# PSUM banks ahead of the scan: seven in turn in place of three

## The chip, the core and the metric

The kernel runs on one core of a Trainium2 chip. Five engines work side by side and wait for one another through semaphores: PE (TensorE, matmuls, with its weight loads shown as PEld), DVE (VectorE), ACT (ScalarE), POOL (GpSimd) and SP (SyncE, which here only starts DMAs). Each engine takes its own instructions strictly in the order in which the program lists them. Matmul results land in PSUM, [...] a tile of 128 x 512 fills one bank. POOL works on SBUF alone in this kernel; PE writes the banks, and DVE and ACT read and write them.

The metric is device time in microseconds (us), the median of several runs. A profile is one further execution with the hardware profiler on.

## What is computed

Eight sequences of 512 tokens and 128 channels pass an adaLN-modulated Mamba2 stack of four layers, and then an adaLN-modulated mixture of eight experts (two per token, and one shared). What matters here is the Mamba part:

```python
h = _layernorm(x) * (1 + ca) + sa                # per sequence, ca and sa from a small matmul
for l in range(4):
    zxbcdt = rmsnorm(h, block_w[l]) @ W_in[l]
    z, xBC, dt = split(zxbcdt)                   # 256, 512 and 8 channels
    xBC = silu(conv_b + sum(pad(xBC)[:, k:k+L] * conv_w[:, k] for k in range(4)))
    xs, Bm, Cm = split(xBC)
    dt = softplus(dt + dt_bias);  dA = exp(dt * -exp(A_log))
    # scan over the tokens: hs = hs * dA + (dt * xs) B;  y = hs C
    h = h + rmsnorm((y + D * xs) * silu(z), gate_w) @ W_out[l]
```

## The kernel before

The scan is done in chunks of 128 tokens. A **unit** is one layer of one sequence (32 of them, layer by layer, eight sequences each); a unit has four chunks, the **items** (128 in all). One hand-written loop (L995) issues everything in program order, one pass for each value of `t`. In pass `t` item `t` is scanned, and the preparation runs ahead by 16 passes: `p = t + 16` counts the passes of preparation, with unit `v = p // 4` and block `j = p % 4`. The first pass is `t = -25` (`p = -9`); up to `t = -1` nothing is scanned, and only preparation runs. That is the stretch which the change touches.

What the preparation of a unit does, by pass:

- **Entry** (`enter`, L614, only for layer 0; a generator stepped once per pass, started at `p = 4b - 9` for sequence b). The modulation matmul into a bank `pmA` (L618), copied out by ACT (L620, L621). Statistics on DVE (L164, L166). For b = 1 to 4 the layernorm itself is on POOL (L149, L150, L172, L185, L186); for the others ACT and DVE do it. Then squares on ACT (L155), the rms factor on POOL (L149, L150), the scaled rows `hn` (POOL L201 for b = 1 to 4), the transposes into a bank `ptA` (L208), and `hT` by ACT (L210).
- **Projection** (`project_x`, L636): in each pass of the unit one block `px` of 128 channels into a bank (L640). ACT makes the first tap of the convolution out of it in the same pass (`conv_first`, L652); DVE adds the other three taps in the next pass (`conv_tap`, L662, three instructions), and only then is the bank free. I write px(v,j), first tap (v,j) and taps (v,j) below.
- `project_z` (L646): two banks `pz`, issued one pass after the unit's last block, and read by ACT one pass later (`silu`, L674, L675).
- `project_dt` (L684): bank `pdt` in the unit's second pass, read by DVE (L689).
- **Softplus** of a group of two units, written out as arithmetic on DVE: stages `softplus_a` (ACT, L697, L698), `softplus_b`, `softplus_c`, `softplus_d` (DVE, L708 to L742), of which b, c and d each take a bank as scratch (`spb`, `spc`, `spd`).
- **Sums** (`sums_a` L750 to L752 on PE into a bank `pc`; `sums_b` L758 to L769), which end with a DMA of the decays to DRAM (`crow`, L767, SP).
- The scan needs that DMA: four passes ahead of its item `decay_rows` (L781) reads `crow` back, broadcast over the partitions, into `dV`; then POOL subtracts and masks (L795, L800), and ACT takes the exponential (L811).

Besides, `prepare_experts` (L254) takes one bank (`pmods`) at `p = 0` for the modulation of the experts.

All the banks just named come from one helper, `pbank` (L504), and one pool of three banks, `psP`. The other five banks belong to the scan: `psX` one (L582; transposes and grams), `psY` two (L583; the chunk outputs `py`, L860) and `psO` two (L584; the output projection `po`, L946). A pool hands out the bank whose last reader comes earliest in the program, and the first instruction that writes the new tile waits for that reader. `psY` is first asked for at `t = 0`, `psO` at `t = 2`.

Of the kernel before, what the change touches and what calls it, by code (L numbers as in the profile page):

```python
# [8 lines left out]
F32 = mybir.dt.float32  # L9
# [6 lines left out]
P = 128  # L16
# [8 lines left out]
def adaln_mamba_moe(  # L25
# [91 lines left out]
    def load_small():  # L117
        with nc.allow_non_contiguous_dma(reason="small parameters, laid out once"):
            nc.sync.dma_start(
                dtb.rearrange("p l h -> p (l h)"),  # L120
                dt_bias.rearrange("l h -> (l h)").partition_broadcast(P),
            )
            nc.sync.dma_start(
                negA.rearrange("p l h -> p (l h)"),
                A_log.rearrange("l h -> (l h)").partition_broadcast(P),
            )
            yield
            for q in range(HB):
                nc.sync.dma_start(
                    Dch[q * HD : (q + 1) * HD],  # L130
                    D.rearrange("l (k q) -> q l k", q=HB)[q].partition_broadcast(HD),
                )
            nc.sync.dma_start(gw, gate_w.rearrange("l (k p) -> p l k", p=P))
            yield
            nc.sync.dma_start(fw, final_w.partition_broadcast(P))
            nc.sync.dma_start(nw, ffn_w.unsqueeze(1))
# [117 lines left out]
    def prepare_experts(pool):  # L254

        pm = pbank("pmods")
        nc.tensor.matmul(pm[:B, : 4 * DM], sc, wm[:, 2 * DM :], start=True, stop=True)
        pv = pm[:B, : 4 * DM].rearrange("p (k d) -> p k d", d=DM)
        mod, mag = (pool.tile([P, NH, Q], F32, tag="dV", name=n)[:, :4, :DM] for n in ("mod", "mag"))
        yield  # L260
        nc.scalar.activation(mag[:B, :2, :], pv[:, 0:4:3, :], AF.Abs)
        nc.scalar.copy(mod[:B, 1, :], pv[:, 1, :])
        nc.scalar.activation(mod[:B, 2, :], pv[:, 2, :], AF.Copy, bias=1.0)
        nc.vector.tensor_scalar(mag[:B, 2:, :], pv[:, 0:4:3, :], 0.0, 2.0, ALU.is_ge, ALU.mult)

        nc.gpsimd.iota(rank, pattern=[[-1, E]], base=E, channel_multiplier=0, **exact)
        nc.gpsimd.iota(base, pattern=[[ER, E]], base=0, channel_multiplier=0, **exact)
        yield
        nc.vector.tensor_scalar_max(mag[:B, :2, :], mag[:B, :2, :], 0.25)
        for k in range(2):  # L270
            nc.vector.scalar_tensor_tensor(
                mod[:B, 3 * k, :], mag[:B, 2 + k, :], -1.0, mag[:B, k, :], ALU.add, ALU.mult
            )
        nc.gpsimd.tensor_sub(below, upto, ident)
        nc.gpsimd.iota(tok, pattern=[[L, 2], [1, NC]], base=0, channel_multiplier=NC, **exact)
        yield
        nc.vector.tensor_mul(mod[:B, 0, :], mod[:B, 0, :], fw[:B])
        yield
        nc.sync.dma_start(mods, mod[:B])
        yield  # L280
        with nc.allow_non_contiguous_dma(reason="small parameters, laid out once"):
            nc.sync.dma_start(rwT, router_w.rearrange("e d -> d e"))
            nc.sync.dma_start(b1[:, :E, :], eb1.rearrange("e (k p) -> p e k", p=P))
            nc.sync.dma_start(b1[:, E, :], sb1.rearrange("(k p) -> p k", p=P))
        nc.sync.dma_start(b2, sb2.partition_broadcast(P))
        yield
# [213 lines left out]
    psP = front.enter_context(tc.tile_pool(name="psP", bufs=3, space=PSUM))  # L500

    wip = front.enter_context(tc.tile_pool(name="wip", bufs=2, side="right"))

    def pbank(name):  # L504
        return psP.tile([P, 512], F32, tag="p", name=name)

    banks.append(pbank)

# [63 lines left out]
    with ExitStack() as actx:  # L572
# [10 lines left out]
        psY = actx.enter_context(tc.tile_pool(name="psY", bufs=2, space=PSUM))  # L583
        psO = actx.enter_context(tc.tile_pool(name="psO", bufs=2, space=PSUM))  # L584
# [22 lines left out]
        def load_x(b):  # L607
            if b % 2 == 0:
                xp[b // 2] = fx.tile([P, 2, NC, DM], F32, tag="x", name=f"x{b}")
                hp[b // 2] = stay.tile([P, 2, NC, DM], F32, tag="h", name=f"h{b}")  # L610
            xs[b] = xp[b // 2][:, b % 2]
            nc.sync.dma_start(xs[b], x[b].rearrange("(s p) d -> p s d", p=P))
# [379 lines left out]
                    del gens[key]  # L992

        EARLY = 9
        for t in range(-NC * LEAD - EARLY, NI + 4):  # L995
            p = t + NC * LEAD
            drain = p >= NI
            if 0 <= p + EARLY < B:
                load_x(p + EARLY)
            if p == 4 - EARLY:  # L1000
                gens["small"] = load_small()
            if p == 0:
                gens["experts"] = prepare_experts(df)
            if t == 2 * NC:
                gens["lists"] = clear_lists()
            if t == NI - LEAD * NC + 2:
                for k, w in enumerate((sw1, sw2.rearrange("(k p) o -> p k o", p=P))):
                    w12.append(wip.tile([P, NPROJ], F32, tag="Wi", name=f"ws{k}")[:, :FH])
                    dst = w12[k] if k == 0 else w12[k].rearrange("p (k o) -> p k o", o=DM)
                    nc.sync.dma_start(dst, w)  # L1010
            for g, seqs in enumerate(sets):
                if t == NC * (U - B) + NC * (seqs[-1] + 1) + 2:
                    gens["pairs", g] = rejoin(g)
            v, j = divmod(p, NC)
            vc, jc = divmod(p - 1, NC)

            if (p + 2 * NC) % (NC * B) == 0 and unit(p // NC + 2):
                load_weights((p // NC + 2) // B)
            if p % (NC * B) == NC and unit(v):
                scale_weights(v // B)  # L1020
            if p == NC:
                nc.scalar.activation(negA, negA, AF.Exp)
                nc.scalar.mul(negA, negA, -1.0)
            if (p + EARLY) % NC == 0 and 0 <= (p + EARLY) // NC < B:
                gens[(p + EARLY) // NC] = enter((p + EARLY) // NC)
            if t % NC == 3 and unit(t // NC - 1) and t // NC - 1 + B < U:
                gens[t // NC - 1 + B] = renorm(t // NC - 1)

            if item(t + 4):
                decay_rows(t + 4)  # L1030
            vz, jz = divmod(p - 5, NC)
            if jz == 0 and unit(vz):
                silu(vz)
            if item(t + 2):
                decay_exp(t + 2)

            if item(t):
                state_out(t)
            if item(t - 1):
                chunk_out(t - 1)  # L1040
            if item(t):
                state_decay(t)
            if item(t + 1):
                weigh(t + 1)
            if drain and scatters and item(t + 3):
                scatter(*scatters.pop(0)[1:])
            if item(t):
                mix(t)
            if item(t - 3):
                out_add(t - 3)  # L1050
            if item(t):
                state_next(t)
            if drain:
                step_pairs()
            if item(t - 1):
                gate(t - 1)
                square(t - 1)
            if item(t - 2):
                project_out(t - 2)
            if item(t + 1):  # L1060
                gram(t + 1)
            if item(t + 2):
                transposes(t + 2)
            if item(t + 3):
                decay_diff(t + 3)
                decay_mask(t + 3)
            if unit(vc):
                conv_tap(vc, jc, 1)
            if item(t - 2):
                out_scale(t - 2)  # L1070
            if unit(vc):
                conv_tap(vc, jc, 2)
                conv_tap(vc, jc, 3)
                px.pop((vc, jc))
            for key in list(gens):
                if not step(gens[key]):
                    del gens[key]
            if drain and routed:
                serve()
            group_stages(p, ((sums_a, 7),))  # L1080
            if j == 1 and unit(v):
                project_dt(v)
            group_stages(p, ((softplus_a, 2), (softplus_b, 3), (softplus_c, 5), (softplus_d, 6), (sums_b, 7)))
            if unit(v):
                project_x(v, j)
                conv_first(v, j)
            if j == 0 and unit(v - 1):
                project_z(v - 1)
# [135 lines left out]
    with tc.manual_schedule(engines={*tc.nc.engines} - {mybir.EngineType.Pool}):  # L1224
# [48 lines left out]
        for b in range(B):  # L1273
# [3 lines left out]
            y = y1[b].rearrange("p (s d) -> p s d", d=DM)  # L1277
# [56 lines left out]
```

## Time and profile before

| | us |
|---|---|
| median of three runs (1149.92 to 1153.31) | 1150.44 |
| the profiled execution, as timed | 1151.86 |
| its span, from the first to the last instruction | 1150.2 |

Busy time in the span, by engine and by stage (us from the span's start):

| stage | length | PE | DVE | ACT | POOL |
|---|---|---|---|---|---|
| 0 to 23, loads and the first entries | 23 | 7.7 | 5.6 | 8.4 | 15.0 |
| 23 to 50, units 0 and 1 | 27 | 16.1 | 19.4 | 18.3 | 24.0 |
| 50 to 77, units 2 and 3, softplus and sums of the first group | 27 | 20.7 | 20.7 | 18.6 | 12.0 |
| 77 to 105, last passes of preparation, first items | 28 | 15.2 | 17.2 | 17.9 | 26.3 |
| 200 to 700, the scan | 500 | 460.3 | 433.4 | 417.7 | 436.7 |
| 830 to 1150, experts and output | 320 | 254.5 | 172.6 | 110.9 | 155.4 |

The first matmul of item 0 (L872) starts at 88.89. How to read the views used later: a line of the waits says which engine and line waited, for whom, and then the total in us, the number of times and the longest. A line of the timeline has the start, the duration of the merged run, engine, line, operation, the tiles written and read, how many instructions were merged (x3), and in brackets how long the engine was idle before it, and who ended that.

### The profile page before, as it was taken

How to read it: one execution, taken by the hardware profiler on the slowest of the kernel's cores; microseconds unless marked ns; L12 is line 12 of the kernel's file. 1: busy time of each engine (PE TensorE's matmuls, PEld its weight loads, DVE VectorE, ACT ScalarE, POOL GpSimd, SP SyncE). 2: the span in 40 equal slices, each digit the busy share in tenths (PEclk: the TensorE clock that was granted, in tenths of full speed). 3: DMA queues.
4: the chain of work that ended last, by engine and by line, in shares of the span. 5: the costliest groups of instructions: out<-in, count | busy, mean ns of one | idle time of the engine just before them, and what ended most of it. 6: DMA issues, size and time to landing. Idle time of an engine off the chain costs nothing. (4 is left out here: it accounts for less than half of the span.)

```text
span 1150.2 us, 21566 instructions
## 1 busy us (share of the span) xinstructions
PE 967.3 (84%) x7130; PEld 732.4 (64%) x7130; DVE 859.0 (75%) x2084; ACT 761.5 (66%) x1641; POOL 856.3 (74%) x937
## 2 busy tenths in 40 slices
PE   3666899989999989999998999879664994999995
PEld 1234666767677667676676676657453674888882
DVE  2858888888988888888889888887764652666653
ACT  3766888878898788888978887876534741333320
POOL 6858879888898798988988988989666163555550
PEclk9777989999999999999999999986886896999998
DMA  5131436455475454653432433423201015788856
GB/s 110 4 128 49 136 98 195 130 157 176 112 227 153 127 183 135 184 170 100 128 109 88 140 109 125 134 91 129 85 27 37 9 45 160 222 231 224 220 145 226
DMA packets 134302, 151.19 MB, mean 131 GB/s; under 512 B 22568, under 2 KB 106696, under 8 KB 134192
## 3 DMA queue, kind: packets, MB, share of 16 engines
q1 hardware_dynamic: 127184, 137.91, 40.6%
q0 software_dynamic: 4672, 9.42, 2.4%
q10 hardware_dynamic: 2336, 2.50, 0.7%
q8 instruction: 56, 0.92, 0.3%
q14 instruction: 54, 0.44, 0.1%
HBM read 120.07 MB, written 29.71 MB: 130 GB/s over the span
## 5 line engine op out<-in xcount | busy, mean ns | idle before, releaser
L662 DVE SCALAR_TENSOR_TENSOR xbc<-px,cw,xbc 128x511 f32<-128x511 f32 (+2 forms) x384 | 286.2, 745 | 36.4 <-ACT xbc L652 29.3
L795 POOL TENSOR_TENSOR dV<-dV,cum 128x1024 f32<-128x1024 f32 x128 | 243.8, 1905 | 5.5 <-DMA dV<-crow 5.5
L854 DVE TENSOR_TENSOR dV<-dV,ptx 128x1024 f32<-128x1024 f32 x128 | 155.1, 1211 | 18.7 <-ACT xT L832 18.7
L800 POOL TENSOR_SCALAR_AFFINE_SELECT dV<-dV 128x1024 f32<-128x1024 f32 x128 | 142.6, 1114 | 9.3
L811 ACT ACTIVATE dV<-dV 128x1024 f32<-128x1024 f32 x128 | 134.5, 1051 | 15.6 <-POOL dV L800 15.3
L487 POOL DMA_INDIRECT yg<-y,ix x78 | 84.1, 1079 | 79.3 <-DVE y L1220 64.7
L938 ACT ACTIVATE sq<-g 128x256 f32<-128x256 f32 x128 | 53.0, 414 | 119.5 <-DVE g L934 105.6
L640 PE MATMUL px<-hT,Wi 128*128 128x512 f32 x192 | 104.9, 629 | 15.8 <-DVE xbc L662 14.5
L652 ACT ACTIVATE xbc<-px,cbias,cw 128x512 f32<-128x512 f32 x128 | 98.4, 769 | 23.3 <-PE px L640 21.9
L838 POOL TENSOR_TENSOR xd<-xT,dt 128x256 f32<-128x256 f32 x128 | 79.5, 621 | 29.4 <-ACT xT L832 28.8
L487 POOL DMA_INDIRECT xg<-row,ix x64 | 63.3, 990 | 50.4 <-ACT hds L523 29.7
L863 PEld LDWEIGHTS py<-xbc,st 128*128 128x128 f32 x384 | 60.3, 204 | 60.6 <-issue 47.4
L953 PE MATMUL po<-Wo,g 128*128 128x128 f32 x512 | 88.9, 297 | 0.0
L1202 ACT ACTIVATE hd<-ph,bs 128x256 f32<-128x256 f32 x78 | 32.7, 470 | 84.1 <-PE ph L1196 81.7
L922 PE MATMUL py<-dV,xd 128*32 128x128 f32 x2048 | 84.5, 284 | 0.0
L949 PEld LDWEIGHTS po<-ones,sq 128*128 128x128 f32 x512 | 67.7, 192 | 26.1 <-issue 23.2
L912 PEld LDWEIGHTS py<-xbc,dg 128*128 128x128 f32 x512 | 79.3, 201 | 7.0 <-issue 1.0
L850 PE MATMUL ptx<-xbc 128*128 128x128 f32 x256 | 56.0, 301 | 32.6 <-DVE dV L854 32.0
L912 PE MATMUL py<-xbc,dg 128*128 128x128 f32 x512 | 81.4, 284 | 0.0
L949 PE MATMUL po<-ones,sq 128*128 128x1 f32 x512 | 78.2, 257 | 0.5 <-ACT sq L938 0.5
L1209 PE MATMUL pe<-w,hd 128*128 128x128 f32 x624 | 75.9, 275 | 0.0
L1196 PE MATMUL ph<-xt,w 128*128 128x256 f32 x312 | 75.8, 388 | 0.0
(252 smaller groups left out, 2348.8 us busy)
## 6 DMA issues: line engine op xcount, KB each, us to landing
dV<-crow SPq DMA_DIRECT2D x128, 512.0 KB, 4.0
w<-in_L_ffn_ew_dram SPq DMA_DIRECT2D x78, 256.0 KB, 3.5
xg<-blank SPq DMA_DIRECT2D x64, 260.0 KB, 4.7
ecum<-crow SPq DMA_DIRECT2D x256, 48.0 KB, 3.2
rows<-xg SPq DMA_DIRECT2D x39, 130.0 KB, 3.2
b<-in_L_ffn_eb_dram SPq DMA_DIRECT2D x39, 64.0 KB, 4.5
x<-in_L_attn_x_dram SPq DMA_DIRECT2D x8, 256.0 KB, 5.4
md<-mods SPq DMA_DIRECT2D x8, 256.0 KB, 4.9
```

What stands on the lines that cost most here:

```text
L487: i = nc.gpsimd.indirect_dma_start(out=to, out_offset=bass.IndirectOffsetOnAxis(ap=ix, axis=0), in_=of, in_offset=None)
L640: nc.tensor.matmul(px[v, k][:, :L], Wi[l][:, c0 : c0 + P], hT[v], start=True, stop=True)
L652: nc.scalar.activation(xbc[v][:, k, :], px[v, k][:, :L], AF.Identity, bias=cbias[:, l, k : k + 1], scale=cw[:, l, k, KT - 1 : KT],)
L662: nc.vector.scalar_tensor_tensor(xbc[v][:, k, d:], px[v, k][:, : L - d], cw[:, l, k, KT - 1 - d : KT - d], xbc[v][:, k, d:], ALU.mult, ALU ...
L795: nc.gpsimd.tensor_tensor(dV[i], dV[i], cums[g][:, h0 : h0 + NH].unsqueeze(2).to_broadcast([P, NH, Q]), ALU.subtract)
L800: nc.gpsimd.affine_select(out=dV[i], in_=dV[i], pattern=[[0, NH], [1, Q]], compare_op=ALU.is_ge, fill=-200.0, base=0, channel_multiplier=-1,)
L811: nc.scalar.activation(dV[i], dV[i], AF.Exp)
L854: nc.vector.tensor_mul(Ms[i], Ms[i], pg.pop(i).unsqueeze(1).to_broadcast([P, NH, Q]))
L912: nc.tensor.matmul(py[i][:, k, :], dg[l][:, k, :], xbc[u][:, k, t], start=False, stop=True, skip_group_check=True,)
L922: nc.tensor.matmul(py[i][j * HD : (j + 1) * HD, k, :], xd[:, h, :], M[:, h, :], start=False, stop=True, skip_group_check=True,)
L949: nc.tensor.matmul(pp[:, 2 * DM + c : 2 * DM + c + 1], sq[:, k, :], ones[:, 0:1], start=(k == 0), stop=(k == NB - 1))
L953: nc.tensor.matmul(pp[:, c * DM : (c + 1) * DM], g[:, k, :], Wo[l][:, k, :], start=(k == 0), stop=(k == NB - 1))
```

## The change

`pbank` looks at a list, `spare`. While the list holds entries, it takes the pool at its head, gives the tile that pool's tag, and moves the entry to the end. The list is filled just before the loop with P, Y, O, P, Y, O, P (for `psP`, `psY`, `psO`), so the three, two and two banks of these pools are asked for in a fixed turn of seven. It is emptied at the start of pass `t = -3` (`p = 13`); from there on every bank comes from `psP` as before. No arithmetic, no instruction and no order of instructions on an engine differs; what differs is the bank that a tile lies in, and so which earlier reader its writer waits for.

```diff
+    spare = []
+
     def pbank(name):
-        return psP.tile([P, 512], F32, tag="p", name=name)
+        pool, tag = psP, "p"
+        if spare:
+            pool, tag = spare[0]
+            spare.append(spare.pop(0))
+        return pool.tile([P, 512], F32, tag=tag, name=name)
...
         EARLY = 9
+        three = ((psP, "p"), (psY, "y"), (psO, "o"))
+        spare.extend((*three, *three, three[0]))
         for t in range(-NC * LEAD - EARLY, NI + 4):
             p = t + NC * LEAD
             drain = p >= NI
+            if t == -3:
+                spare.clear()
```

## The prediction

> **What bounds the kernel now.** Only the passes before t = -3 change, so I read the 40 slices first, then the waits of each engine from 23 to 77.3 us, then the timelines of DVE, ACT and POOL there.
>
> From the page's slices (28.8 us each, busy share in tenths):
>
> ```profile
> DVE  2858888888988888888889888887764652666653
> POOL 6858879888898798988988988989666163555550
> ```
>
> POOL is at 6, 8, 5, 8 in the first four slices: nearly full from 29 to 58, half empty from 58 to 86. So the stretch has two halves with different limits. The waits of 23 to 77.3:
>
> ```profile
> PE px L640 <- DVE xbc L662: 8.1, 3, 4.7
> PE pdt L684 <- ACT mdA L621: 3.3, 1, 3.3
> ...
> ACT xbc L652 <- PE px L640: 9.2, 6, 4.0
> ACT unread L155 <- POOL h L186: 3.3, 2, 2.9
> ...
> POOL dtd L769 <- ACT edec L765: 6.8, 1, 6.8
> POOL dV L795 <- DMA dV<-crow: 5.5, 1, 5.5
> ```
>
> PE does wait for banks: a new px for the taps that still read an old one, and ACT then waits for that px. But ACT also waits for POOL's layernorm, and the last two rows are the hole of the second half: POOL sits idle until the first group's sums reach it, first as edec, then through DRAM as dV. POOL's timeline gives the places:
>
> ```profile
> 50.87 0.19 POOL L149 TENSOR_SCALAR rrA<-ssA 128x4 f32<-128x4 f32 x1 [1.83 <-ACT unread L155]
> ...
> 61.97 1.27 POOL L186 TENSOR_TENSOR h<-h,mdA 128x512 f32<-128x512 f32 x1
> 70.03 0.32 POOL L769 TENSOR_TENSOR dtd<-dt,edec 128x64 f32<-128x64 f32 x1 [6.79 <-ACT edec L765]
> ...
> 77.24 1.90 POOL L795 TENSOR_TENSOR dV<-dV,cum 128x1024 f32<-128x1024 f32 x1 [5.51 <-DMA dV<-crow]
> ```
>
> From 23.84 to 49.04 POOL has no gap that matters (23.95 busy in 25.25): entries 1 to 3 back to back, needing no bank that is late. From 77.24 to 97.5 it is full again (19.50 of 20.30), now with the scan. **The start of the scan is the arrival of dV at 77.24.** What moves that moves the end; what moves only PE does not.
>
> **The path to 77.24, backwards.** dV lands 4.0 after its issue at 73.23; that follows the crow DMA, issued at 69.73. Before it ACT copies the sums (67.88), loads a table (1.28) and takes exponentials; it waited for DVE's edec (L760, 67.56). And DVE:
>
> ```profile
> 48.66 2.31 DVE L662 SCALAR_TENSOR_TENSOR xbc<-px,cw,xbc 128x511 f32<-128x511 f32 x3 [0.64 <-ACT xbc L652]
> ...
> 58.96 0.19 DVE L689 TENSOR_TENSOR v<-pdt,dtb 128x32 f32<-128x32 f32 x1 [0.85 <-PE pdt L684]
> ...
> 61.27 2.32 DVE L662 SCALAR_TENSOR_TENSOR xbc<-px,cw,xbc 128x511 f32<-128x511 f32 x3 [0.92 <-ACT xbc L652]
> ...
> 67.56 0.23 DVE L760 TENSOR_TENSOR edec<-pc,cum 128x64 f32<-128x64 f32 x1
> ```
>
> From 48.66, taps (1,2), to 67.79 DVE is busy but for two gaps, 0.85 and 0.92. So three places can give: the start at 48.66 and these gaps.
>
> **The change, part by part.** It adds and removes no instruction. I followed each tile through the turn P, Y, O, P, Y, O, P with the release order of each pool.
>
> *The start, taps (1,2).* They need first tap (1,2), which ACT ends at 48.63. ACT runs without another gap from 36.62 to there but for one:
>
> ```profile
> 40.03 0.78 ACT L652 ACTIVATE xbc<-px,cbias,cw 128x512 f32<-128x512 f32 x1 [0.53 <-PE px L640]
> ...
> 54.86 0.78 ACT L652 ACTIVATE xbc<-px,cbias,cw 128x512 f32<-128x512 f32 x1 [2.06 <-PE px L640]
> ...
> 60.47 0.77 ACT L652 ACTIVATE xbc<-px,cbias,cw 128x512 f32<-128x512 f32 x1
> ```
>
> px(1,0) waited for taps (0,2), which ended at 37.8; in the turn it takes the bank of px(0,0), read by 27.1, so its matmuls run near 32 and 0.53 goes. Earlier nothing is won: at 35.01 ACT's squares wait for POOL's h (2.90), and POOL is full from 23.84. The 4.03 that ACT waited for px(0,1) at 29.33 goes, but comes back in front of these squares. First tap (1,2) ends at 48.1: **0.53**.
>
> *The gap of 0.85, pdt of unit 2.* It waited for the bank of px(2,0), read until 58.1. In the turn it takes that of px(1,2), read until 48.13 + 2.25 = 50.4. DVE asks for it after spb (1.70), taps (1,3) 2.25, statistics 1.14 and taps (2,0) 2.25, at 57.7. **0.85** goes.
>
> *The gap of 0.92, first tap (2,1).* ACT, from its squares of entry 3 (end 50.77, set by POOL's h at 49.04): first tap (1,3) to 51.45, the copies of pmA 0.45 (waited 0.91), first tap (2,0) 0.78 (waited 2.06), table load 1.28, two z activations 1.1 (0.62 between them), the silu of xBC 1.9, first tap (2,1) 0.78. Without the three waits it ends at 57.7. Taps (1,3), which the silu needs, end at 54.2. DVE gets to taps (2,1) at 57.7 + 0.2 + 1.2 = 59.1, so 1.4 to spare. **0.92** goes.
>
> The sum: 0.53 + 0.85 + 0.92 = **2.30**. edec ends at 65.5 in place of 67.79, crow is issued at 67.4 and POOL starts the scan at 74.9.
>
> *What is late next.* DVE, without a gap from 48.1 to 65.5. Close behind is POOL: its rsA of entry 4 waits for DVE's statistics, now ready at 55.45 for 55.98; h is done at 62.7 for 63.24, ACT's squares (1.7) at 64.4, and the copy of the sums follows them. So even a DVE without work would let ACT begin the sums at 64.4 for 67.88: **3.5 is the most** that this stretch can give.
>
> *The other banks* cost nothing. The scratch banks of softplus are free well ahead. After t = -3, pdt of unit 3 takes the bank of pc, px(3,1) that of the first pz of unit 2, the transposes of entry 4 that of px(3,0), and from there the turn of psP is as before. The first py takes the bank of px(2,3), read until about 70.6, and is wanted at 86.6: 16 us of cover.
>
> [...] Taken as the size of the gain it would be all of PE's bank waits from 23 to 77: 8.1 + 3.3 + 1.9 + 1.0 + 0.5 + 0.4 + 0.4 = 15.6, a time of 1134.8. The row of POOL decides: PE is not what the scan waits for. [...] PE, no longer held up, does its work in a bunch and idles longer before the next hn. The trace has both rates: a px of 2.05 at 37.95, after 4.74 idle, and of 1.10 at 48.17. On my path lie only the sums (1.7 at 65.10), which run beside taps (2,2) (2.25). Were they slower by 1.0, 0.4 would show and the sum be 1.9; I keep 2.3, since they come now too after 2.1 idle.
>
> **What becomes of 2.3 after 77.** In the first passes of the scan everybody follows POOL (DVE's 7.62 before 87.46 goes back through ACT to POOL's work from 77.24), so the shift is whole. Between 0 (a later wait for something not moved) and 2.3 I take 2.3: work and order behind are the same, and every DMA there is issued by the chain itself. Against the profiled execution, span 1150.2, that is 1147.9; against the median, 1150.44, **1148.1**. That is 0.2%, under the 0.3% (3.5 us) that a measurement can tell from no change.
>
> **The rivals.**
> - *More comes off*: POOL's spans are rough, and if its chain before 63 is looser than shown, ACT decides from 40 on. Its waits for px and pmA there, 0.53 + 0.91 + 2.06 + 1.22, are 4.7: 1145.7. For it: these waits are real. Against: the cap of 3.5.
> - *Nothing arrives*: the gain meets slack in the scan or in the experts' stage, where the chain that ended last is full of transfers of rows (3% of the span). 1150.4. Against: 15 more crow rounds, none with a fixed time.
> - *Slower*: the granted clock. From 960 to 1125 PE is busy 151 of 165 us at a granted 0.97 and carries the chain; [...] the clock has been at 0.75 to 0.81 in other stages. At 0.93 this one costs 151 x (0.97/0.93 - 1) = 6.5 more: 1150.44 - 2.3 + 6.5 = 1154.6. Below 0.955 it outweighs the gain. Against: PE's work is the same and moves by a few us.
>
> **How the numbers follow.** Forecast 0.55 (own range 1146.8 to 1149.8, from the cap and a lost half), more 0.23, nothing 0.13, slower 0.09. Low is 1145.0, just under the first rival; high is 1151.6, the second plus the spread of the runs. Faster by over 0.3% takes most of the first rival and a fifth of the forecast, 0.32; slower 0.09; the rest, 0.59, within.
>
> **What would show it.** PE's waits for DVE xbc before 77 nearly gone; ACT's for px small but at 30 to 37, where the squares' wait grows; POOL's timeline the same to 50; DVE without gaps from 48.1 to 65.5; POOL's first L795 at 74.9, its wait for dV still about 5.5; item 0's L872 at 86.6. Wrong if the first L795 comes before 73.7 or at 77, or if it comes at 75 and the end does not follow.

## The result, and the profile after

| | before | after |
|---|---|---|
| median (lowest to highest), four runs each on the same chip | 1150.81 (1149.92 to 1153.31) | 1143.28 (1141.50 to 1145.30) |
| the profiled execution, as timed | 1151.86 | 1141.50 |
| its span | 1150.2 | 1139.8 |
| DVE's edec, start | 67.56 | 65.01 |
| crow DMA, issued | 69.73 | 67.18 |
| SP goes on to dV, after the issue of crow | 3.50 | 2.17 |
| POOL's first L795 (now L801) | 77.24 | 73.52 |
| item 0's L872 (now L878) | 88.89 | 85.17 |
| POOL's last L795 (now L801) | 839.65 | 829.89 |

The ratio is 0.9945, with a 95% interval of 0.9923 to 0.9967: 7.5 us faster by the medians, where 2.3 were forecast. (In the two profiled executions the spans differ by 10.4.) Line numbers of this stretch are 6 higher after the change. In what follows, runs more than 1.5% above the fastest of their kernel count as slow and are left out of means and ratios, but not of the medians (of the experiments below, two runs each of e1, e6 and e13, one of e14); with them the leads of e1 and e6 would be 3.0 and 3.4 in place of 3.9 and 4.0.

The two rows of the slices that were shown of before, from the page of after:

```profile
DVE  3768888898888978988889889888764652666653
POOL 6868879898898898988988988879756163555550
```

In the third slice (57 to 86 us) DVE is at 6 for 5 and POOL at 6 for 5: the hole ahead of the scan has become shorter. Such a row shows no more than that. DVE's timeline of after has the four instructions to which the prediction gave a time:

```profile
48.07 2.32 DVE L668 SCALAR_TENSOR_TENSOR xbc<-px,cw,xbc 128x511 f32<-128x511 f32 x3 [0.64 <-ACT xbc L658]
...
57.44 0.18 DVE L695 TENSOR_TENSOR v<-pdt,dtb 128x32 f32<-128x32 f32 x1
...
58.73 2.31 DVE L668 SCALAR_TENSOR_TENSOR xbc<-px,cw,xbc 128x511 f32<-128x511 f32 x3
...
65.01 0.23 DVE L766 TENSOR_TENSOR edec<-pc,cum 128x64 f32<-128x64 f32 x1
```

The second and the third row have no bracket any more: the idle times of 0.85 and 0.92 in front of them are gone, and taps (1,2) start 0.59 earlier. POOL's timeline of after, the same rows as before:

```profile
50.87 0.19 POOL L149 TENSOR_SCALAR rrA<-ssA 128x4 f32<-128x4 f32 x1 [1.83 <-ACT unread L155]
...
61.37 1.26 POOL L186 TENSOR_TENSOR h<-h,mdA 128x512 f32<-128x512 f32 x1
...
67.49 0.32 POOL L775 TENSOR_TENSOR dtd<-dt,edec 128x64 f32<-128x64 f32 x1 [4.85 <-ACT edec L771]
...
73.52 1.90 POOL L801 TENSOR_TENSOR dV<-dV,cum 128x1024 f32<-128x1024 f32 x1 [4.33 <-DMA dV<-crow]
```

To 50.87 it is the same to a few hundredths. Then the gain comes in two steps: the wait for edec falls by 1.94 (6.79 to 4.85, and h is 0.6 earlier), and the wait for dV by another 1.18. The waits of after from 23 to 77.3 (total, times, longest):

```profile
ACT unread L155 <- POOL h L186: 9.5, 3, 4.4
...
POOL dtd L775 <- ACT edec L771: 4.9, 1, 4.9
POOL dV L801 <- DMA dV<-crow: 4.3, 1, 4.3
...
ACT xbc L658 <- PE px L646: 1.2, 2, 1.0
```

The 8.1 us in which PE's px waited for DVE's taps are gone from this list, and ACT's 9.2 for px have shrunk to 1.2. Most of that came back as ACT's wait for POOL's h, which grew from 3.3 to 9.5. So 15.6 us of bank waits bought 2.55 us of edec.

In the scan the lead changes. By POOL's subtractions, one for each item, it is 3.7 at item 0, 4.7 from item 15, 5.7 from item 31 and 6.8 from item 55 to item 109: three single steps of about 1.1 us, with flat stretches between. Over the last 18 items it goes up and down (8.4, then 6.0 at item 124) and ends at 9.8. The step near 390, from PE's timeline of before in the pass of one item:

```profile
387.39 0.96 PE L684 MATMUL pdt<-Wi,hT 128*128 128x8 f32 x8
388.81 1.92 PE L640 MATMUL px<-hT,Wi 128*128 128x512 f32 x2 [0.46 <-DVE xbc L662]
390.52 1.06 PE L863 MATMUL py<-xbc,st 128*128 128x128 f32 x4
391.37 1.06 PE L872 MATMUL py<-xe,xT 128*128 128x256 f32 x2
```

and of after, in the same pass:

```profile
381.68 0.96 PE L690 MATMUL pdt<-Wi,hT 128*128 128x8 f32 x8
383.09 1.12 PE L646 MATMUL px<-hT,Wi 128*128 128x512 f32 x2 [0.46 <-DVE xbc L668]
384.05 0.61 PE L869 MATMUL py<-xbc,st 128*128 128x128 f32 x4
384.50 0.60 PE L878 MATMUL py<-xe,xT 128*128 128x256 f32 x2
```

The instructions and the wait of 0.46 are the same, but in before the same matmuls take 1.92, 1.06 and 1.06 instead of 1.12, 0.61 and 0.60. Two of the 2.5 us windows of before around it (length; busy time of PE, PEld, DVE, ACT, POOL; granted clock; DMA share; GB/s) show what changed:

```profile
390.00:392.50 2.50, 2.50 (x9) 1.80 (x9) 1.72 (x5) 2.39 (x5) 2.43 (x3) 0.52 0.04 15
392.50:395.00 2.50, 2.50 (x34) 2.18 (x34) 2.22 (x5) 0.42 (x1) 0.71 (x1) 1.00 0.21 25
```

By the clock's own records PE was granted half its clock from 389.00 to 392.41, and then the whole of it. The profile of after has such episodes too, fewer (13 windows of 3.41 us at half its clock from item 5 on, for 17) and partly in other passes.

### The profile page after: what moved, and what is told of

Its sections match the earlier page's. It is cut to its first block, busy times and chain, and to the rows that moved or that the text cites. A ratio compares the mean times of both kernels' runs of the same rounds, so it can differ in the third digit from the quotient of the medians.

```text
span 1139.8 us, 21562 instructions
## 1 busy us (share of the span) xinstructions
PE 960.9 (84%) x7130; PEld 730.6 (64%) x7130; DVE 855.0 (75%) x2084; ACT 761.4 (67%) x1641; POOL 856.1 (75%) x937
## 5 line engine op out<-in xcount | busy, mean ns | idle before, releaser
L801 POOL TENSOR_TENSOR dV<-dV,cum 128x1024 f32<-128x1024 f32 x128 | 244.7, 1912 | 4.5 <-DMA dV<-crow 4.3
```

The costliest lines, as they stand in the source:

```text
L801: nc.gpsimd.tensor_tensor(dV[i], dV[i], cums[g][:, h0 : h0 + NH].unsqueeze(2).to_broadcast([P, NH, Q]), ALU.subtract)
```

## The experiments

Three theories stood at the outset. **Start**: the scan begins earlier, the whole of this arrives at the end, and what goes beyond it is chance. **Scan**: the other banks also change something later. **Clock**: the lead over the start is a matter of when PE gets its full clock. The runs of four batches were on other chips than the first result, with before at 1168.6 to 1171.1 us in place of 1150.8; each is compared with runs of before on its own chip.

### Is it the start, and which banks? (e1 to e4)

e1_after_again is the changed kernel without an edit. e2_after_mask3 puts the start of the scan back by work on POOL alone, by computing the first mask of the decays three times more, with the same values:

```diff
+                if t == -3:
+                    for _ in range(3):
+                        decay_mask(t + 3)
```

e3_before_mask3 is the same edit in before. e4_from_p8 takes seven banks only from `p = 8`, so that units 0 and 1, and the entries beside them, still have three:

```diff
-        spare.extend((*three, *three, three[0]))
...
+            if p == 8:
+                spare.extend((*three, *three, three[0]))
```

> The changed kernel once more, for a tighter interval and a second profile. Shift theory (the end moves by what the scan's start moves, and the rest of the 7.5 us was chance): the first subtraction of item 0 on POOL again near 73.5 in place of 77.24, the ratio settles near 1 - 3.7/1150.8 = 0.9968. Gate theory (the rest is how often PE falls to half rate in the scan, in short episodes that cost about 1.1 each in the first trace pair, and these move with the start): below 0.9968, near 0.9945 again if the pattern is tied to this program, and the second profile shows steps of about 1.1 against before at matmuls that run at half rate. Bank theory (psP is left in another turn, and the scan itself is faster): below 0.9968, and the lag against before grows evenly through the scan.

> The changed kernel with item 0's mask done three times more on POOL (1.1 each, same values): the scan starts 3.3 later, about where it started before the change. Shift theory: 3.3 above the changed kernel, 1146.6 if that stays at 1143.3. Bank theory: the same 1146.6, and so 4 below before although the scan starts within 0.5 of it. Gate theory: not the changed kernel plus 3.3 but anything from 1145 to 1151, with half-rate episodes in the scan at other places.

> The kernel before with item 0's mask done three times more on POOL: the scan starts 3.3 later. Shift and bank theory: 3.3 above before, 1154.1 (ratio 1.0029). Gate theory: the number of half-rate episodes changes, so anything from 1149 to 1157; a time at or below before's would show that a later start alone can be worth as much as an earlier one.

> Half of the change: the turn of seven only from p = 8 to p = 12, three banks ahead of that. My sum has 0.53 of the 2.3 before p = 8, and 0.85 + 0.92 after: the crow DMA is issued 1.8 earlier than before, at about 68.0, DVE without gaps from 50.9 to its edec. Shift theory: 1.8 plus whatever the DMA itself gains (1.3 in the first pair, if that is tied to the change and not chance), so 1147.7 to 1149. Gate theory: the same start, but the end anywhere from 1143 to 1151. If PE's bank waits before p = 8 carry most of the gain, nothing is left: 1150.8.

| | edec | SP goes on after crow | first L795 | first L872 | median | ratio to before, 95% |
|---|---|---|---|---|---|---|
| before, same chip, 67 runs | | | | | 1169.18 | |
| e1_after_again, 22 | 65.08 | 2.17 | 73.47 | 85.15 | 1166.31 | 0.9968 [0.9949, 0.9987] |
| e2_after_mask3, 14 | 65.09 | 2.17 | 73.64 | 88.81 | 1168.26 | 1.0005 [0.9978, 1.0031] |
| e3_before_mask3, 22 | 67.66 | 2.17 | 76.06 | 91.18 | 1172.33 | 1.0020 [1.0000, 1.0041] |
| e4_from_p8, 22 | 67.16 | 2.17 | 75.72 | 87.37 | 1164.15 | 0.9961 [0.9940, 0.9983] |

(L795 and L872 are L801 and L878 in the kernels made from after.) From e1 to after the stretch ahead of the scan repeats to a tenth, but the end gives 3.9 ± 0.9 us (means 1165.1 and 1169.0; behind ± stands the standard error here and below), not 7.5. With the start put back to 88.8, e2 is level with before, which starts item 0 at 88.89 in its first profile: the means are 1168.0 and 1169.0, 1.0 ± 0.9 apart. Moving the start by POOL's work moves the end in the same direction in both programs, as the start theory has it.

e4 does not fit. Its edec is only 0.4 earlier than in before and 0.5 than in e3, and its first L795 is 2.2 later than after's, and yet it ends like after (mean 1165.2). How its edec got late is in its ACT timeline:

```profile
53.20 0.27 ACT L626 COPY mdA<-pmA 128x128 f32<-128x128 f32 x1 [1.47 <-PE pmA L624]
...
54.91 0.78 ACT L658 ACTIVATE xbc<-px,cbias,cw 128x512 f32<-128x512 f32 x1 [1.26 <-PE px L646]
```

With three banks for the passes ahead of `p = 8`, its copies of pmA still wait 1.47, and first tap (2,0) another 1.26, since px(2,0) queues behind pmA on PE. So the gain needs the banks of the earlier passes as well. Why the end did not suffer from the later start is open.

e3 told something else. In before, by PE's timeline, the two z blocks of the first unit took this long:

```profile
39.79 2.40 PE L646 MATMUL pz<-hTA,Wi 128*128 128x512 f32 x4
```

and in e3, whose program is the same up to there:

```profile
39.80 3.62 PE L646 MATMUL pz<-hTA,Wi 128*128 128x512 f32 x4
```

In before the clock's records have PE at half its clock from 37.42 to 40.83, and px(1,0), at 37.95 behind a wait of 4.74 for a bank, took 2.05. In e3 it took 2.05 as well, behind a wait of 4.16, and pz came at 3.62, where it takes 1.88 in after at a granted clock of 1.00: by these lengths the half rate lasted through pz. In e4 px(1,0) took 2.04 and pz 3.62, too. In e3 ACT's silu of z waited 0.72 for it, and taps (1,2) started at 49.51, not at 48.66. The gaps in front of the two later DVE instructions were smaller in exchange (0.58 and 0.46), and edec came at 67.66 against 67.56. How the 2.3 us are divided over the three places is thus not fixed; the sum nearly is.

### How far does before agree with itself, and is it the tail? (e5 to e8)

e5_before_again and e6_after_third are before and after without an edit. e7_before_cut and e8_after_cut are before and after without the eight experts, the gathering of tokens and the sum of their outputs:

```diff
-        for rest in fetched:
-            rest()
...
-            nc.vector.tensor_add(xs[b], xs[b], y)
+        for b, g in enumerate([fold(b) for b in range(B)]):
+            finish(g)
```

> The kernel before, against itself: 1.000. Both theories. How far from 1 it comes out is what chance alone does to a ratio here; if it is off by 0.003, the 5 us that the first result and e4 have beyond their earlier scan start need no cause in the program. Its profile: the first subtraction of item 0 on POOL at 75.7 to 76.1 if the crow DMA takes 2.2 until SP goes on, at 77.2 if it takes 3.5 again.

> The changed kernel on the chip of e5. Shift theory: item 0's first subtraction at 73.5, so 2.5 earlier than before with an equal crow DMA, and a ratio to before near 0.9978, whatever chance adds in either direction. If something of the program beyond the start makes 5 us more, the ratio is near 0.994 again while e5 is at 1.000.

> The kernel before without the experts' stage: it ends once the tokens are routed and the shared expert is added, and leaves out the eight experts, the gathering of their results and their sum. This takes away the stage whose length differed most between profiles (310 to 334). Some 940 in place of 1150. Only its difference to e8 counts.

> The changed kernel without the experts' stage (the same is left out as in e7). Shift theory: 2.5 below e7, and the runs of both spread by steps of about 1.1 for half-rate episodes in the scan. Gate theory, where the program decides the episodes: 5 to 7 below e7. Profiles: the intervals between the first subtraction of successive items equal in both but for single steps of about 1.1.

| | edec | SP goes on after crow | first L795 | last L795 | median | runs |
|---|---|---|---|---|---|---|
| before, same chip | | | | | 1169.37 | 35 |
| e5_before_again | 67.45 | 2.17 | 75.78 | 838.12 | 1173.25, ratio 1.0013 [0.9984, 1.0042] | 14 |
| e6_after_third | 65.02 | 2.17 | 73.77 | 830.67 | 1167.35, ratio 0.9966 [0.9941, 0.9991] | 22 |
| e7_before_cut | 67.53 | 3.45 | 77.08 | 835.87 | 1026.52 (1024.33 to 1030.79) | 6 |
| e8_after_cut | 65.02 | 2.17 | 73.73 | 834.70 | 1022.66 (1018.27 to 1026.11) | 6 |

The same program against itself is 2.0 us off in the mean (1171.95 and 1169.9), inside the interval. That is the measure for everything here: after is ahead by 4.0 ± 1.2 us in the mean, or by 4.6 when e5's runs are counted with those of before, and a difference of 2 us between two kernels is not to be read. Without the experts the lead is 4.9 ± 1.7 us in the means, so it doesn't need the experts' stage. My estimate of the length of the cut kernel was some 85 us too short; for the comparison this doesn't matter.

e5 also shows the program of before with the short crow transfer, as e3 had: three banks can have it too. SP's timeline of e5:

```profile
69.61 0.70 SPq L767 DMA_DIRECT2D crow<-ct  x1
71.79 0.82 SPq L781 DMA_DIRECT2D dV<-crow  x2
```

### What does an even earlier start bring? (e9 to e12)

e9_exp_early has an exponential of one column, whose result nobody reads, ahead of ACT's wait for the statistics, so that the table load (1.28) comes off the path between edec and crow:

```diff
+            if p == 11:
+                nc.scalar.activation(unread[:, 0:1], mhalf[:, 0:1], AF.Exp)
```

e10_after_cut_mask2 is e8 with two masks more at `t = -3`; e11_before_cut_again and e12_after_cut_again are e7 and e8 without a further edit.

> The changed kernel, and ACT takes one exponential of a column at the start of pass p = 11, so that the table load of 1.28 which stood between the group's edec and its decays falls into ACT's idle time ahead of POOL's h (4.10 idle before 62.67 in the changed kernel). The path from edec to the crow DMA is shorter by 1.28: crow issued at 65.9 in place of 67.18, item 0's first subtraction at 72.3 in place of 73.5. If DVE's edec is what bounds this stretch, as I say, all of it shows at the start; if POOL's h and ACT's squares bind (end 64.37), too, since the copy of the sums waits for 65.24 anyway. The time: 1.3 under the changed kernel, ratio to before near 0.9967.

> The changed kernel without the experts' stage, item 0's mask done twice more on POOL (2 x 1.1): the scan starts 0.3 before that of the kernel before with an equal crow DMA. Shift theory: equal to e11 within 0.5, apart from episodes of half rate. If the changed kernel has an advantage beyond its earlier start, it stays 2 or more below e11.

> The kernel before without the experts' stage, a second set of runs on the chip of e10 and e12. Item 0's first subtraction at 75.8 or, with the long crow DMA, at 77.1; 1026.5 as in e7 if this chip is like that one.

> The changed kernel without the experts' stage, a second set. Shift theory: 2.5 to 3 below e11 (2.5 of DVE's gaps, and half of the time 1.3 of the crow DMA). First set: 4.85 by the means of six runs each.

| | edec | SP goes on after crow | first L795 | last L795 | median | runs |
|---|---|---|---|---|---|---|
| before, same chip | | | | | 1168.60 | 23 |
| e9_exp_early | 65.03 | 2.39 | 72.27 | 830.41 | 1162.36, ratio 0.9960 [0.9941, 0.9979] | 18 |
| e10_after_cut_mask2 | 65.18 | 2.17 | 73.80 | 833.37 | 1024.92 | 6 |
| e11_before_cut_again | 67.35 | 3.62 | 77.35 | 840.56 | 1024.37 | 6 |
| e12_after_cut_again | 65.04 | 2.17 | 73.61 | 835.74 | 1017.90 | 6 |

In e9 the load moves where ACT was idle anyway. From its ACT timeline:

```profile
58.59 1.28 ACT L1032 ACT_TABLE_LOAD   x1
59.88 0.20 ACT L1032 ACTIVATE unread<-mhalf 128x1 f32<-128x1 f32 x1
62.69 0.31 ACT L155 ACTIVATE unread<-h 128x128 f32<-128x128 f32 x1 [2.60 <-POOL h L186]
```

It fills part of the wait for POOL's h, which was 4.10 in after. The crow DMA goes out at 65.80 for 67.18, by SP's timeline of e9, and POOL starts the scan 1.25 earlier:

```profile
65.80 0.70 SPq L773 DMA_DIRECT2D crow<-ct  x1
68.19 0.82 SPq L787 DMA_DIRECT2D dV<-crow  x2
```

In the mean e9 is 5.0 ± 1.0 us faster than before on its chip. It is the earliest start of the study; its lead over after in the whole time was not measured on one chip.

Without the experts after is ahead by 5.8 ± 1.75 us in the means (e12 against e11). With its start put back (e10, first L878 at 87.77, where e11's L872 is at 89.00) nothing of it can be seen: the mean is 0.3 above e11's, though with a standard error of 2.2. Together with e2 this speaks against an effect of the banks later on. So does DVE's trace: of its instructions ahead of the experts only two, the first ones of spb (50.90) and spc (59.07), wait for other semaphores than in before.

e11 issues crow within 0.1 us of e5, and its program is the same up to there. SP's timeline of e11:

```profile
69.52 0.70 SPq L767 DMA_DIRECT2D crow<-ct  x1
73.14 0.82 SPq L781 DMA_DIRECT2D dV<-crow  x2
```

Here SP got on 3.62 after the issue, and in e5 2.17 after it. What else the DMA engines moved between 66 and 75 tells the two apart. Each number is the rate in a fortieth of these 9 us, first in before, which has the long transfer too (3.50), then in e5; the row of a queue has its packets and MB:

```profile
GB/s 0 0 0 0 0 0 0 0 0 0 0 0 0 0 0 0 0 0 0 0 0 73 50 178 46 0 0 7 9 2 0 0 0 0 0 0 127 255 419 328
...
q8 instruction: 1, 0.02, 0.9%
```
```profile
GB/s 0 0 0 0 0 0 0 0 0 0 73 0 0 0 0 0 0 0 0 0 0 0 155 137 0 0 0 0 0 0 200 364 346 255 237 164 273 218 310 328
...
q8 instruction: 1, 0.02, 0.6%
```

The lone 73 is one packet of 16 KB of the queue that the profile calls `instruction`; by this name alone I take it for a piece of the program, and call it a fetch of instructions. The group around 155 or 178 is crow, and the last one dV. In e5 the packet ran from 68.33 to 69.25, before crow was issued. In before it ran from 70.89 to 72.18, and 8 of crow's 128 packets of 512 B (the 7, 9 and 2) started only at 72.17. It is so in all eighteen profiles: in the five with a long transfer the last 8 packets of crow start within 0.02 us of the end of such a packet, and in the other thirteen none overlaps with crow's packets. So **crow is long when it meets a fetch of instructions**. With three banks the fetch came at 68.3 to 71.1 us, and crow, issued at 69.5 to 69.8, met it in five of seven profiles; with seven banks, or seven from `p = 8`, it came at 63.5 to 68.3 and met crow in none of eleven. What sets the moment of the fetch no run here shows.

On the clock theory the clock records of the traces say more. In all of them the granted clock changes only on a grid of 3.41 us. The program does not fix where the grid lies: modulo 3.41 its lines are at 3.29 and 1.82 us from the first instruction in before and e5, which are one program, and at 3.24, 0.57 and 0.49 in after, e1 and e6, which are another. Ordered by where the grid lies against the scan, the profiles of four layers are:

| grid line after item 4's L795 | profiles (banks) | half rate begins just before the L795 of items (5 to 112) | item 4's L795 to the last |
|---|---|---|---|
| -0.18, 0.09, 0.13 | e12 (7), e5 (3), before (3) | 5, 11, 15, 29, 53, 109, in each | 740.6, 740.8, 740.9 |
| 0.28 | e3 (3) | 5, 11, 13, 109 | 738.0 |
| 0.39 | after (7) | 5, 11, 13, 111 | 734.9 |
| 0.71 | e6 (7) | 5, 11, 13, 45, 85 | 735.4 |
| 0.78, 0.81, 0.83 | e4 (7 from `p = 8`), e10 (7), e2 (7) | 5, 11, 13, 45, 101, in each | 735.6, 735.8, 735.9 |
| 1.14, 1.24 | e1 (7), e8 (7) | 5, 11, 15, 85; 5, 11, 15, 53, 61, 101 | 736.0, 739.5 |
| 1.83, 1.85 | e11 (3), e9 (7) | 5, 11, 15, 93; 5, 11, 15 | 741.7, 736.6 |
| 2.48 | e7 (3) | 5, 11, 13, 61, 101 | 737.3 |

The first row has both programs, at the same place of the grid within 0.31 us: the half rate falls on the same items, and the scan takes the same time within 0.3 us. One of these episodes, that ahead of item 53, in the windows of before, e5 and e12 (granted clock 0.50 in each):

```profile
389.00:392.41 3.41, 3.41 (x9) 2.20 (x9) 2.57 (x7) 3.31 (x8) 2.77 (x3) 0.50 0.29 103
```
```profile
387.53:390.94 3.41, 3.41 (x10) 2.19 (x10) 2.58 (x8) 3.35 (x8) 2.81 (x3) 0.50 0.28 100
```
```profile
385.05:388.46 3.41, 3.41 (x9) 2.19 (x10) 2.58 (x8) 3.29 (x8) 2.74 (x3) 0.50 0.28 99
```

So with the grid at the same place the banks make no difference to the scan, and the **scan** theory falls. The first pair was in part luck: e12 is the program of after up to there, and its scan is 5.8 longer than after's, which is the shortest of all. Not everything follows the grid: e1 and e8 lie close together and differ by 3.5, and e11 and e9 by 5.1, most of it in the last 16 items. Over all rows the five scans with three banks take 739.7 in the mean and the eight with seven 736.8, 2.9 ± 1.1 apart; from fourteen profiles at scattered places of the grid it can't be told whether that is chance.

### One layer alone (e13 to e16)

In a short program a start that is 2.5 to 3.3 us earlier must show, and the scan has a quarter of the passes in which anything can be added. e13_before_layer1 and e15_before_layer1_again are before with one layer, e14_after_layer1 and e16_after_layer1_again are after, and all leave out three layers, the routing and the experts:

```diff
-        U = NL * B
+        U = B
...
```

> The kernel before with one layer of the Mamba stack in place of four, ended after the scan of that layer: the three other layers, the routing, the experts and the final sums are left out, and h is written out as it stands. About 300. Only its difference to e14 counts.

> The changed kernel, the same left out as in e13. If the lead is the start and the rest accrues along the scan: 2.5 to 3.3 below e13 by the means (2.5 from DVE's gaps, 0.8 from the crow DMA where it was long in 3 of 5 profiles, little from a quarter of the scan). If the whole lead belongs to the start: 5 below e13.

> e13 once more, for the spread between two sets of the same kernel: equal to e13 within 1. The crow DMA's time until SP goes on, 2.2 or 3.5, in another profile.

> e14 once more: equal to e14 within 1, and 2.5 to 3.3 below e15, or 5 if the whole lead belongs to the start.

| | edec | SP goes on after crow | first L795 | median | runs |
|---|---|---|---|---|---|
| e13_before_layer1 | 67.63 | 3.92 | 77.85 | 274.89 | 6 |
| e15_before_layer1_again | 67.40 | 3.23 | 77.30 | 276.11 | 5 |
| e14_after_layer1 | 66.42 | 2.19 | 75.01 | 272.43 | 5 |
| e16_after_layer1_again | 64.98 | 2.19 | 73.52 | 271.54 | 5 |

Over nine runs of each program, the means are 274.6 and 271.5: 3.15 ± 0.7 us. That agrees with what the start gives (3.3 by the means of the first L795), without anything beyond it. (In e14's profile all is 1.4 later from 27 us on, ahead of the stretch in question.)

## Why the prediction was right or wrong

- **What bounds the kernel** and **where the gain is made**: right. DVE's start at 48.66 and the two gaps were the three places. 2.30 was the sum; edec measures 2.55 in the first pair, of which 0.59, 0.85 and 0.92 are the three places, and the rest small change. The waypoints came within 0.4: taps (1,2) at 48.07 for 48.1, pdt's reader at 57.44 for 57.7, taps (2,1) at 58.73 for 59.1, POOL's h done at 62.63 for 62.7, edec's end at 65.24 for 65.5. ACT's squares ended at 64.4 as said, and the sums were copied after edec, at 65.34, so the cap of 3.5 was not reached.
- **PE's bank waits taken as the size of the gain**: refuted with their own number, 15.6 us of waits for 2.55.
- **The half rate, held against the change**: after has it behind a wait, as was said: PE waited 6.40 ahead of the transposes at 42.27, with half its clock from 37.38 to 47.62. What counted lies on the other side. With three banks PE waited 4.1 to 4.7 ahead of px(1,0), which took 2.04 to 2.05, and the pz at half rate behind it (3.62) was on the path to taps (1,2) in e3 and e4. In after, where PE had not waited there (px(1,0) took 1.02 and pz 1.88), they started at 48.07. That the waits bring the half rate about was the author's estimate; these runs show the two together.
- **The DMA from crow to dV**: the first term that failed. "edec ends at 65.5 in place of 67.79, crow is issued at 67.4 and POOL starts the scan at 74.9" carries the 3.50 between crow and dV along as fixed. It was 2.17 after, so L801 came at 73.52, below the 73.7 at which the prediction called itself wrong. In before, crow's last packets had waited for a fetch of instructions; after the change the fetch lies ahead of crow. By these profiles (none of eleven against five of seven) this is an effect of the change that the sum doesn't have, worth 1.3 in the first pair; since three banks escape it in two profiles of seven, it is about 1 on the average. The mean of the first L795 is 76.95 in the seven profiles with three banks and 73.63 in eight of after (without e9, and without e14, which was late before the stretch): 3.3 us.
- **The shift is whole**: the second step that failed, in "What becomes of 2.3 after 77". "Work and order behind are the same" is right, and the start arrives at the end: 3.15 ± 0.7 in one layer, 3.9 ± 0.9 in e1, 4.0 ± 1.2 in e6, 1.0 ± 0.9 in e2, where it was put back. But the prediction took from this that the scan takes the same time, and so gave its length no term. From the first L795 to the last it took 762.4 in before and 756.4 in after, 6.0 less, with 13 windows of 3.41 us at half rate from item 5 on against 17. Over all profiles of four layers it took 758.8 to 763.2 us in five with three banks and 756.4 to 762.1 in eight with seven (the added masks taken off); after and e12, the same program up to there, differ by 5.7. The range, whose low end lay 5.4 us under the median of before, rested on three runs with 3.4 us between them and had no room for it. Of the 7.5 us, about 3.3 are the start; the rest goes with the clock in the scan, and chance alone can make it. The standard deviation is about 4 us among runs of one kernel in the larger sets, so a difference of four against four has a standard error of some 2.8, and 7.5 lies 1.5 of these above 3.3.
- **The rivals**: *more comes off* named a size (4.7) near the lead over all batches (4.3, below) and a wrong place: edec came only 2.55 earlier, so ACT's waits did not add to the start. *Nothing arrives* is refuted. *Slower* is refuted in its sign. It had, alone among them, the granted clock in hand, which is where most of the rest lies, though it looked for it in the experts' stage and not in the scan. In that stage (960 to 1100) the clock was 0.97 in before and 1.00 in after. That an earlier start moves the clock was the author's estimate.

Of the three theories the start is shown and the scan has fallen; of the clock it is shown that one program gets scans up to 5.7 apart, while whether the earlier start has a bearing on it stays open. The leads in the means of e1, e6, e8 and e12, weighted by their errors, give 4.3 ± 0.6, 1.6 standard errors above the 3.3 of the start. Open, too, is e4: 3.8 ± 0.95 ahead of before with a start that is only 1.2 earlier than the mean of three banks. Something of 2 us in these times isn't understood.

## What to carry to other kernels

To size a gain from more buffers, find the engine whose idle hole ends at the start of the next stage, and walk the chain that fills it; here the waits for buffers on another engine mostly turned into waits for something else (15.6 us became 2.55). A duration seen once, such as that of a DMA round trip (crow to dV took 3.50 in one execution of before and 2.17 in another), is a sample: before it is carried into a forecast as fixed, look for its other values, and for other packets (here a fetch of instructions) in the same time. And run the old kernel against itself before reading a few tenths of a per cent: here that alone gave 1.0013.

## What was not expected of the hardware

- **Half rate without a long idle time.** In the scan of before PE was busy for 92% of the time (460.3 of 500 us from 200 to 700), and yet fell to half its clock for 3.41 us from 389.00, just behind a wait of 0.46, and in another execution of the same passes, that of after, it did not. Such an episode in mid-scan costs about 1.1 us. Ahead of px(1,0) the half rate had stood beside a wait of 4.74; in the 3.41 us right in front of this episode, 385.59 to 389.00, PE was busy for 2.95 us by the profile, at a granted clock of 1.00. What makes the clock fall is thus not shown by these runs. The grid of 3.41 us on which it changes has another place from one execution of a program to the next (modulo 3.41, 3.29 in before and 1.82 in e5).
- **A longer time goes with a lower mean clock.** Over 67 runs of before on one chip, from 1159.4 to 1176.8 us, time and mean granted clock (about 0.922) correlate with -0.74, at 0.76 us for 0.001 of clock. e5's 2.0 us against itself shrink to 0.5 ± 1.0 at the same clock; e1 keeps 3.8 ± 0.7 and e6 4.4 ± 0.7. The correction may not be free of the effect: whether the mean clock depends in its turn on how long PE waits, no run shows.
- **A fetch of instructions holds up data.** From the issue of crow to that of dV, which waits for it, SP needed 2.17 to 2.19 in twelve profiles, 2.39 in e9, and 3.2 to 3.9 in the five in which a packet of 16 KB of the queue `instruction` (0.9 to 1.5 us) lay in crow's way, for the same transfer on the same queue.
